# A scan's output in two passes with the next layer's row transform in the same stream, and that layer's first half transformed back beside its second half's items

## The chip, the cores and the metric

The kernel runs on one core of one Trainium2 chip. The metric is device time in microseconds (us), the median of the runs of one kernel.

## The reference, cut to what matters

Four layers follow each other on one image of 48 x 48 tokens with 768 channels, all in float32: attention with an MLP, a Fourier layer, a scan over 12 iterations, and a second Fourier layer. The change touches the last step of the scan and the second Fourier layer.

```python
# end of the scan layer
Hg = C_rot * Hst
Ho = transpose(Hg).reshape(B, H, W, R * N)          # R * N = 256
x = silu(Ho @ W_out + b_out)                        # 256 -> 768
# second Fourier layer
xs = rfft2(x, axes=(1, 2))                          # along h and w
# 8 blocks of 96 channels: two complex products with relu between, softshrink
x = irfft2(out_c, s=(H, W), axes=(1, 2)) + x
```

## The kernel before, in words

Tile code builds the kernel: the program is written as a sequence of operations on tiles, a scheduler orders them on each engine by the place where they are written and by the buffers that come free, and it inserts the waits. The order of each engine is then fixed.

**Scan output (`scan_phase`, lines 1223 to 1246).** The state `hg` has positions along w on the partitions; one column of `NPR` = 24 holds a pair of image rows. For two pairs at a time (`p2`, 12 rounds) four PE transposes (L1234) write a PSUM tile `ht`, ScalarE copies it to `hT` (L1236), and then for each of the two pairs and each half of the 768 channels (384 each) two matmuls (L1243, tile `so`, two passes each in the records) are followed by the addition of the bias on VectorE (L1245, tile `st`) and Silu on ScalarE into `x3` (L1246). `x3` has 96 partitions (two image rows of 48), 24 pairs and 768 channels. PSUM is split into two banks for `ht` and six for `so`.

**Second Fourier layer (`afno_second`, from L1561).** It has its own pools, opened when the scan's are closed. First, `spectrum_rows` (L1353) transforms along w: for each half of the channels and each of six groups of four pairs, four matmuls with the constant `fw` (L1361, tile `f_f`), four copies out of PSUM (`Evac`, L57 on ScalarE and L59 on VectorE in turn) into `ys` (two buffers), and one store of `ys` to DRAM, `yu[half]`, issued by SP (L1363).

Then `spectrum_mix` (L1366) loads its parameters (six of them, SP), sums two of them on GpSimd (L1402, L1403), and works through 40 items: two halves, five chunks of five frequencies (`kc`), four blocks of 96 channels. For each chunk it loads `yt` from `yu` (L1393, three buffers) and at the chunk's end stores `us` into the same place of `yu` (L1477). An item has four stages, each a few steps behind the one before: `s_fft_h` (five matmuls L1420 into `f_x`, copy L1422 on ScalarE, sum L1424 on GpSimd), `s_mlp1` (three matmuls L1434 to L1436, VectorE and ScalarE work, L1445 on GpSimd), `s_mlp2` (ten matmuls L1455 and L1456, two VectorE operations L1459 and L1461) and `s_ifft_h` (one matmul L1470 and a copy into `us`). A step of the loop runs them for four different items, in this way:

```python
stages = {s_ifft_h: 4, s_mlp2: 3, s_mlp1: 1, s_fft_h: 0}
for step in range(len(items) + 4):
    for stage, behind in stages.items():
        if 0 <= step - behind < len(items):
            stage(step - behind)
    beside(step)
```

`beside` is a callback; the first Fourier layer uses it for other work, the second gives one that does nothing. After all items, the transform back along w runs (L1582 to L1594): for each half and each of six groups, `load_spectrum` reads four pairs of `yu[half]` into `gt` (L1491, four buffers, SP); a group needs the `us` of all five chunks of its half. Four matmuls with `iw` follow (L1588, tile `f_w`), a VectorE addition onto `x3` in place (L1590) after each, and a store of four pairs to the output, issued by ScalarE (L1594). The last group of each half is stored pair by pair, from ScalarE and SP in turn (L1592). The scheduler places the first loads of the first half's `gt` ahead of the last items already, as far as the four buffers go; the matmuls on them stand behind the last item.

Of the kernel before, what the change touches and what calls it, by code (L numbers as in the profile page):

```python
# [11 lines left out]
F32 = mybir.dt.float32  # L12
BF16 = mybir.dt.bfloat16
AF = mybir.ActivationFunctionType
ALU = mybir.AluOpType
AX = mybir.AxisListType
PSUM = bass.MemoryType.PSUM
DRAM = bass.MemoryType.DRAM

P = 128  # L20
G = 48
# [7 lines left out]
TB = 384  # L29
NTB = T // TB  # L30
# [969 lines left out]
def scan_phase(tc, ident, w, w_close, wts, xT, xT_close, c_d, cr_d, out_open):  # L1000
# [7 lines left out]

    nc = tc.nc
    (b0_d, b1_d, cb_d, bands_d, wo_d, bo_d) = wts
    R4 = 3
# [8 lines left out]
    with tc.tile_pool(name="sc_s", bufs=1, side="left") as sp:  # L1022
# [202 lines left out]
        with (  # L1225
            tc.tile_pool(name="so_t", bufs=3, side="left") as tp,
            tc.tile_pool(name="so_q", bufs=2, space=PSUM) as pt,
            tc.tile_pool(name="so_p", bufs=6, space=PSUM) as pm,
        ):
            for p2 in range(NPR // 2):  # L1230
                ps = pt.tile([P, 512], F32, tag="t", name=f"ht_{p2}")
                for t in range(2):
                    for j in range(2):
                        nc.tensor.transpose(ps[:, (2 * t + j) * P : (2 * t + j) * P + K], hg[:K, 2 * p2 + t, j * P : (j + 1) * P], ident[:K, :K])  # L1234
                hT = tp.tile([P, 4, 2, G], F32, tag="hT", name=f"hT_{p2}")
                nc.scalar.copy(hT, ps.rearrange("p (i s w) -> p i s w", i=4, s=2)[:, :, :, :G])  # L1236
                for t in range(2):
                    pr = 2 * p2 + t
                    for half in range(2):
                        cols = slice(half * TB, (half + 1) * TB)  # L1240
                        ps = pm.tile([P, 512], F32, tag="m", name=f"so_{pr}_{half}")
                        for j in range(2):
                            nc.tensor.matmul(ps[:BS, :TB], lhsT=hT[:, 2 * t + j].rearrange("p s w -> p (s w)"), rhs=wo[:, j, cols], start=j == 0, stop=j == 1)  # L1243
                        t_ = tp.tile([BS, TB], F32, tag="t", name=f"st_{pr}_{half}")
                        V.tensor_tensor(t_, ps[:BS, :TB], bo[:, cols], ALU.add)  # L1245
                        nc.scalar.activation(x3[:, pr, cols], t_, AF.Silu)  # L1246
    return x3


def turn(eng, out, in_, co, si, m):  # L1250
# [12 lines left out]
def block_kernel(ctx: ExitStack, tc: tile.TileContext, a: dict):  # L1263
# [80 lines left out]
    wts = [a[k] for k in ("b_scan", "bias_scan", "conv_b", "bands", "W_out", "b_out")]  # L1344
    c_d = dram.tile([P, 8, NN * RR + 2 * NM, 3], F32, tag="c_d", name="c_d")
    cr_d = dram.tile([P, 8, NN * RR, 3], F32, tag="cr_d", name="cr_d")
    x3 = scan_phase(tc, ident, wsc, wsc_close, wts, x2T, x2T_close, c_d, cr_d, out_open)
    afno_second(tc, a, x3, yu)
    for close in reversed(closes):
        close()  # L1350

# [11 lines left out]
    nc.sync.dma_start(yu[half][:, 4 * g : 4 * g + 4, :], ys)  # L1363


def spectrum_mix(tc, name, a, layer, yu, psum, keep, side, halves, beside):  # L1366

# [2 lines left out]

    nc = tc.nc
    ev = Evac(nc)
    w1, b1, w2, b2 = (a[f"{layer}_{k}"] for k in ("w1", "b1", "w2", "b2"))
    HB = NB // 2
    with (
        tc.tile_pool(name=f"{name}_c", bufs=1, side=side) as cp,
        tc.tile_pool(name=f"{name}_y", bufs=3, side=side) as yp,
        tc.tile_pool(name=f"{name}_s", bufs=2, side=side) as sp,  # L1380
    ):
        fh = cp.tile([BS, BS], F32, tag="fh", name=f"{name}_fh")
        nc.sync.dma_start(fh, a["fh"])
        w1t = cp.tile([BS, NB, 2, BS], F32, tag="w1", name=f"{name}_w1")
        w1s, w1d = (cp.tile([BS, NB, BS], F32, tag=n, name=f"{name}_{n}") for n in ("w1s", "w1d"))
        w2t = cp.tile([BS + 1, NB, 2, BS], F32, tag="w2", name=f"{name}_w2")
        b1t = cp.tile([BS, 2, NB], F32, tag="b1", name=f"{name}_b1")
        ih = cp.tile([BS, BS], F32, tag="ih", name=f"{name}_ih")
        ys = {}

        def load(half, kc):
            yt = yp.tile([BS, KC, TB], F32, tag="yt", name=f"{name}_yt_{half}_{kc}")
            nc.sync.dma_start(yt, yu[half][4 * KC * kc : 4 * KC * (kc + 1)].rearrange("(k q) p c -> (q p) k c", q=4))  # L1393
            us = sp.tile([BS, KC, TB], F32, tag="us", name=f"{name}_us_{half}_{kc}")
            ys[half, kc] = yt, us

        nc.sync.dma_start(w1t, w1)
        nc.sync.dma_start(b1t, b1)
        nc.sync.dma_start(w2t[:BS], w2)
        nc.sync.dma_start(w2t[BS : BS + 1], b2)  # L1400
        nc.sync.dma_start(ih, a["ih"])
        nc.gpsimd.tensor_tensor(w1s, w1t[:, :, 0, :], w1t[:, :, 1, :], ALU.add)  # L1402
        nc.gpsimd.tensor_tensor(w1d, w1t[:, :, 1, :], w1t[:, :, 0, :], ALU.subtract)  # L1403

        o1s = []
        for i in range(3):
# [6 lines left out]
        def s_fft_h(i):  # L1413
            half, kc, b = items[i]
            if b == 0:
                load(half, kc)
            yt = ys[half, kc][0]
            ps = psum(f"x_{i}")
            for j in range(KC):
                nc.tensor.matmul(ps[:BS, j * BS : (j + 1) * BS], lhsT=yt[:, j, b * BS : (b + 1) * BS], rhs=fh, start=True, stop=True)  # L1420
            X = sp.tile([BS, 2, KC, G], F32, tag="X", name=f"{name}_X_{i}")
            nc.scalar.copy(X, ps[:BS, :CH].rearrange("c (k r h) -> c r k h", r=2, h=G))  # L1422
            Xs = sp.tile([BS, KC, G], F32, tag="Xs", name=f"{name}_Xs_{i}")
            nc.gpsimd.tensor_tensor(Xs, X[:, 0], X[:, 1], ALU.add)  # L1424
            flow[i] = X, Xs
# [103 lines left out]
def afno_first(tc, a, yu, x2T, follow_in, load_next):  # L1529

    nc = tc.nc
    ev = Evac(nc)
    x2v = x2T.rearrange("p c (h w) -> p c h w", w=HD)
    nc.gpsimd.memset(x2v[:, :, :, G:], 0.0)
    with (
        tc.tile_pool(name="f1_g", bufs=1, side="right") as gp,  # L1540
        tc.tile_pool(name="f1_p", bufs=8, space=PSUM) as pm,
    ):

        def psum(tag):
            return pm.tile([P, 512], F32, tag="m", name=f"f1_{tag}")

        iw = gp.tile([4 * KW, BS], F32, tag="iw", name="f1_iw")
        follow = follow_in(gp, 1)
        spectrum_mix(tc, "f1", a, "L1", yu, psum, True, "left", (1, 0), lambda step: follow(psum) if step in (1, 4) else load_next() if step == 8 else None)
        nc.sync.dma_start(iw, a["iw"])  # L1550
        for half in (1, 0):
            for g in range(NTB):
                gt = load_spectrum(nc, gp, yu, half, g, "f1", 3)
                for ct in range(NC // 2):
                    ps = psum(f"w_{half}_{g}_{ct}")
                    for i in range(4):
                        nc.tensor.matmul(ps[:, i * BS : (i + 1) * BS], lhsT=gt[: 4 * KW, i, ct * P : (ct + 1) * P], rhs=iw, start=True, stop=True)
                    ev(x2v[:, half * NC // 2 + ct, 8 * g : 8 * g + 8, :G], ps[:, :TB].rearrange("p (h w) -> p h w", w=G))


def afno_second(tc, a, x3, yu):  # L1561

    nc = tc.nc
    ev = Evac(nc)
    out = a["out"].rearrange("(p t) c -> t p c", t=BS)
    with (
        tc.tile_pool(name="f3_g", bufs=1, side="left") as gp,
        tc.tile_pool(name="f3_p", bufs=8, space=PSUM) as pm,
    ):
        fw = gp.tile([BS, YR], F32, tag="fw", name="f3_fw")  # L1570
        nc.sync.dma_start(fw, a["fw2"])
        iw = gp.tile([4 * KW, BS], F32, tag="iw", name="f3_iw")
        nc.sync.dma_start(iw, a["iw"])

        def psum(tag):
            return pm.tile([P, 512], F32, tag="m", name=f"f3_{tag}")

        for half in range(2):
            for g in range(NTB):
                spectrum_rows(nc, fw, x3[:, 4 * g : 4 * g + 4, half * TB : (half + 1) * TB], yu, half, g, psum, gp, ev, "f3")  # L1580
        spectrum_mix(tc, "f3", a, "L3", yu, psum, False, "left", (0, 1), lambda step: None)
        for half in range(2):  # L1582
            cols = slice(half * TB, (half + 1) * TB)
            for g in range(NTB):
                gt = load_spectrum(nc, gp, yu, half, g, "f3", 4)
                for i in range(4):
                    ps = psum(f"w_{half}_{g}_{i}")
                    nc.tensor.matmul(ps[:BS, :TB], lhsT=iw, rhs=gt[: 4 * KW, i, :], start=True, stop=True)  # L1588
                    dst = x3[:, 4 * g + i, cols]
                    nc.vector.tensor_tensor(dst, ps[:BS, :TB], dst, ALU.add)  # L1590
                    if g == NTB - 1:
                        (nc.scalar, nc.sync)[i % 2].dma_start(out[:, 4 * g + i, cols], dst)  # L1592
                if g < NTB - 1:
                    nc.scalar.dma_start(out[:, 4 * g : 4 * g + 4, cols], x3[:, 4 * g : 4 * g + 4, cols])  # L1594

# [109 lines left out]
```

## Time and profile before

| | us |
|---|---|
| median of 3 runs | 3879.38 (3878.82 to 3880.02) |
| the profiled execution | 3878.45 |
| its span, first to last instruction | 3876.6 |
| PE busy | 3761.5, 97% of the span |
| mean granted PE clock | 0.978 |
| stretch of the scan's output and what follows it | 3527 to 3876.6 |

PE matmul and PEld (its weight load) overlap, and matmul ends are modelled: two passes that follow each other overlap in the records, so the distance between starts is what a pass takes. Each instruction is named by engine, source line, operation, the tile it writes and those it reads, and its shape. "Idle before" names what ended the wait. DMA share is the mean busy share of the 16 DMA engines; a granted clock of 0.5 means that PE ran at half speed.

The stages can be followed by their first instructions: transposes of the scan's output at 3527.0, first `f_f` at 3598.8, first `f_x` of the items at 3634.5, last `f_o` at 3821.5, first `f_w` at 3830.75, last addition onto `x3` at 3872.8.

### The profile page before, as it was taken

The page shows a single profiled execution, that of the slowest core. Times are in us where ns is not written, and L with a number is a line of the kernel's source. Part 1 is how long each engine was busy: PE and PEld are TensorE (multiplying, and loading weights), DVE is VectorE, ACT ScalarE, POOL GpSimd, SP SyncE. Part 2 cuts the span into 40 slices and gives each one's busy share as a digit, 9 for nine tenths or more (in the row PEclk, how much of TensorE's full clock was granted, in tenths as well). Part 3 has the DMA queues.
Part 4 walks back from the last instruction along what each step waited for, and adds up shares of the span by engine and source line. Part 5 has one row for each costly group of instructions (what it writes and reads, how often), then busy time and mean ns, then how long its engine had stood idle before and what let it go on. Part 6 is the DMA issues. An engine that isn't in the chain of part 4 may idle for free. (4 is left out here: it accounts for less than half of the span.)

```text
span 3876.6 us, 54460 instructions
## 1 busy us (share of the span) xinstructions
PE 3761.5 (97%) x22018; PEld 2285.7 (59%) x22018; DVE 2059.0 (53%) x3185; ACT 1141.9 (29%) x1907; POOL 658.4 (17%) x496
## 2 busy tenths in 40 slices
PE   8999989999999999998999999999999998999998
PEld 4666544444444444455555555555568866996685
DVE  6655456666666666555425333232335367995355
ACT  1322244444444444421310120021023246223341
POOL 3101011111111111024000000000023301981131
PEclk9999989999999999999999999999999799999999
DMA  7656563424232322134334434433454302110444
GB/s 257 210 187 197 173 183 112 127 92 133 84 110 83 105 87 76 36 95 161 123 105 155 150 107 124 147 122 108 132 139 110 96 24 93 40 32 22 146 108 159
DMA packets 266810, 460.43 MB, mean 119 GB/s; under 512 B 32989, under 2 KB 219349, under 8 KB 260055
## 3 DMA queue, kind: packets, MB, share of 16 engines
q1 hardware_dynamic: 256919, 436.23, 36.3%
q10 hardware_dynamic: 9632, 20.65, 1.4%
q8 instruction: 175, 2.87, 0.3%
q14 instruction: 84, 0.69, 0.1%
HBM read 318.49 MB, written 138.31 MB: 118 GB/s over the span
## 5 line engine op out<-in xcount | busy, mean ns | idle before, releaser
L576 DVE TENSOR_TENSOR acc<-acc,p 128x768 f32<-128x768 f32 x576 | 582.8, 1012 | 354.9 <-ACT p L568 316.5
L568 ACT ACTIVATE p<-s 128x768 f32<-128x768 f32 x648 | 478.5, 812 | 692.7 <-PE s L566 580.5
L929 PE MATMUL p<-w,h 128*128 128x384 f32 x1512 | 492.7, 486 | 0.0
L558 PE MATMUL s<-qt,kv 64*128 64x384 f32 x2592 | 478.5, 501 | 9.1 <-ACT p L568 7.4
L587 PE MATMUL av<-p,kv 128*64 128x384 f32 x2592 | 464.5, 493 | 0.0
L929 PEld LDWEIGHTS p<-w,h 128*128 128x128 f32 x1512 | 286.1, 190 | 196.9
L558 PEld LDWEIGHTS s<-qt,kv 64*128 64x128 f32 x2592 | 233.1, 187 | 249.9 <-ACT p L568 116.0
L587 PEld LDWEIGHTS av<-p,kv 128*64 128x64 f32 x2592 | 170.0, 136 | 225.2 <-issue 215.8
L866 PE MATMUL p<-x2nT,w 128*128 128x384 f32 x864 | 294.0, 490 | 3.1 <-issue 3.1
L294 PE MATMUL qk<-xnT,wqk 128*128 128x384 f32 x756 | 252.5, 491 | 5.2 <-DMA wqk<-wqk_d 5.2
L1172 PE MATMUL c<-H,bands 128*48 128x96 f32 x5632 | 242.8, 247 | 12.1 <-issue 11.5
L566 PE MATMUL s<-bt,oneh 120*128 120x384 bf16 x1296 | 248.3, 328 | 0.0
L1172 PEld LDWEIGHTS c<-H,bands 128*48 128x48 f32 x5632 | 234.2, 123 | 20.9 <-issue 11.9
L866 PEld LDWEIGHTS p<-x2nT,w 128*128 128x128 f32 x864 | 165.4, 192 | 119.1 <-issue 6.0
L866 PE MATMUL p<-xT,w 128*128 128x384 f32 x648 | 220.8, 486 | 0.0
L566 PEld LDWEIGHTS <-oneh 120*128 120x128 bf16 x1296 | 109.1, 98 | 174.3 <-issue 115.1
L294 PEld LDWEIGHTS qk<-xnT,wqk 128*128 128x128 f32 x756 | 144.6, 193 | 99.9 <-issue 8.5
L905 POOL TENSOR_TENSOR rr<-rr,ml_b 128x1152 f32<-128x1152 f32 x12 | 33.5, 2788 | 954.4 <-DMA rr<-xr_d 660.8
L861 ACT ACTIVATE h<-h,ml_b 128x384 f32<-128x384 f32 x144 | 88.3, 614 | 346.6 <-DVE h L881 174.3
L1180 POOL TENSOR_TENSOR t<-s,c 128x768 f32<-128x768 f32 x80 | 144.8, 1836 | 214.3 <-DVE s L1142 203.8
L866 PEld LDWEIGHTS p<-xT,w 128*128 128x128 f32 x648 | 123.1, 190 | 85.9
L1082 PE MATMUL c<-wsc,x2T 128*112 128x357 f32 (+1 forms) x576 | 151.6, 426 | 2.0 <-DVE c L1043 2.0
(314 smaller groups left out, 4778.7 us busy)
## 6 DMA issues: line engine op xcount, KB each, us to landing
w<-w1s_d SPq DMA_DIRECT2D x36, 768.0 KB
w<-w2s_d SPq DMA_DIRECT2D x36, 768.0 KB
bt<-rh_d SPq DMA_DIRECT2D x144, 162.0 KB
w<-w1s_d SPq DMA_DIRECT2D x36, 576.0 KB
w<-in_mlp_w_dram SPq DMA_DIRECT2D x27, 768.0 KB
wqk<-wqk_d SPq DMA_DIRECT2D x12, 1344.0 KB
yu<-f_ys SPq DMA_DIRECT2D x24, 672.0 KB
f_gt<-yu SPq DMA_DIRECT2D x24, 672.0 KB
```

What stands on the lines that cost most here:

```text
L294: nc.tensor.matmul(p[:, :TB], lhsT=w[:, n, c, :], rhs=ops[sb][n][:, c, :], start=c == 0, stop=c == NC2 - 1)
L558: nc.tensor.matmul(ps[:, s, :QB], lhsT=keys[pr % 2][rows, kt * P : (kt + 1) * P], rhs=qbs[qc % 2][0][rows], start=True, stop=False)
L566: nc.tensor.matmul(ps[:, s, :QB], lhsT=oneh[:NBR, b % 3, :], rhs=qbs[qc % 2][1][:NBR, s, b // 3, j, :], start=False, stop=True)
L568: nc.scalar.activation(p, ps[:, :, :QB], AF.Exp)
L576: nc.vector.tensor_tensor(probs[c], probs[c], p, ALU.add)
L587: nc.tensor.matmul(avs[c][rows, :QB], lhsT=vals[pr % 2][:, kt, rows], rhs=p[:, s, :], start=kt == 0, stop=kt == NT - 1)
L861: nc.scalar.activation(h, h, AF.Gelu, bias=b1c[:, k : k + 1])
L866: nc.tensor.matmul(p[:, :TB], lhsT=w[n][:, c, :], rhs=rhs[n][:, c, :], start=c == 0, stop=c == NC2 - 1)
L929: nc.tensor.matmul(ps[t][:, :TB], lhsT=hs[left, f][:, t * P : (t + 1) * P], rhs=wt[:, f % KW2, :], start=f == 0, stop=f == NF2 - 1)
L1082: nc.tensor.matmul(ps[:K, i, :n], lhsT=xT[:, cc, tok : tok + K], rhs=w[:, cc, c0 : c0 + n], start=cc == 0, stop=cc == NC - 1)
L1172: nc.tensor.matmul(ps[r0 : r0 + G, k // 4, cols], lhsT=bands[:, n - GC, i, :] if gr else bands0[:, n, i, :], rhs=H[:, n, :, d : d + NPR], ...
L1180: GP.tensor_tensor(t, sc[:, ch], c1[:, m0 : m0 + GC].unsqueeze(2).to_broadcast([P, GC, RR, NPR]), ALU.mult)
```

## The change

**The scan's output in two passes.** `scan_phase` becomes a generator. The loop over halves goes outside the loop over `p2`: the first pass makes the 12 `hT` tiles (now each with a buffer of its own) and the first half of the channels; the second pass reuses them for the second half. After each `p2` of each pass it yields.

**The rows' transform in the same stream.** `afno_second` starts before the scan's output, opens its parameters and constants first (`spectrum_open`, the part of `spectrum_mix` that loaded them, now on the right side of memory), and at every second yield transforms one group of the rows that are finished, with the scan's six PSUM banks. While the second half's first three groups are transformed, it also writes the first half's three `yt` loads.

**The first half back within the items.** `beside` now loads the first half's `gt` from step 27 on and transforms its six groups back after steps 32, 35, 38, 40, 41 and 42 of 44. Behind the items only the second half's six groups remain. The pair-by-pair store is kept for the very last group alone.

```diff
@@ scan_phase
-            for p2 in range(NPR // 2):
...
+            yield x3, psum
+            hTs = []
+            for half in range(2):
+                cols = slice(half * TB, (half + 1) * TB)
+                for p2 in range(NPR // 2):
+                    if half == 0:
+                        ps = pt.tile([P, 512], F32, tag="t", name=f"ht_{p2}")
...
+                        hT = tp.tile([P, 4, 2, G], F32, tag=f"hT{p2}", name=f"hT_{p2}", bufs=1)
+                        nc.scalar.copy(hT, ps.rearrange("p (i s w) -> p i s w", i=4, s=2)[:, :, :, :G])
+                        hTs.append(hT)
+                    hT = hTs[p2]
+                    for t in range(2):
+                        pr = 2 * p2 + t
+                        ps = psum(f"{pr}_{half}")
                         for j in range(2):
                             nc.tensor.matmul(ps[:BS, :TB], lhsT=hT[:, 2 * t + j].rearrange("p s w -> p (s w)"), rhs=wo[:, j, cols], start=j == 0, stop=j == 1)
                         t_ = tp.tile([BS, TB], F32, tag="t", name=f"st_{pr}_{half}")
                         V.tensor_tensor(t_, ps[:BS, :TB], bo[:, cols], ALU.add)
                         nc.scalar.activation(x3[:, pr, cols], t_, AF.Silu)
-    return x3
+                    yield
@@ spectrum_open (new; the loads were in spectrum_mix)
+    cp, yp = (stack.enter_context(tc.tile_pool(name=f"{name}_{n}", bufs=bufs, side=side)) for n, bufs in (("c", 1), ("y", 3)))
...
+    def load(half, kc):
+        if (half, kc) not in yts:
+            yts[half, kc] = yp.tile([BS, KC, TB], F32, tag="yt", name=f"{name}_yt_{half}_{kc}")
+            nc.sync.dma_start(yts[half, kc], yu[half][4 * KC * kc : 4 * KC * (kc + 1)].rearrange("(k q) p c -> (q p) k c", q=4))
+        return yts[half, kc]
@@ afno_second
+    x3, scan_psum = next(scan)
+    with ExitStack() as stack:
+        opened = spectrum_open(tc, stack, "f3", a, "L3", yu, "right")
...
+        ready = [(half, g) for half in range(2) for g in range(NTB)]
+
+        def rows_in(n, psum):
+            half, g = ready[n]
+            spectrum_rows(nc, fw, x3[:, 4 * g : 4 * g + 4, half * TB : (half + 1) * TB], yu, half, g, psum, gp, ev, "f3")
+            if NTB <= n < NTB + 3:
+                opened[1](0, n - NTB)
+
+        for n, _ in enumerate(scan):
+            if n and n % 2 == 0:
+                rows_in(n // 2 - 1, scan_psum)
+            if n == 4 * NTB - 1:
+                rows_in(2 * NTB - 1, scan_psum)
...
+        items = 2 * NKC * (NB // 2)
+        loads = {items - 13 + 2 * g: g for g in range(4)}
+        backs = {items - 8: 0, items - 5: 1, items - 2: 2, items: 3, items + 1: 4, items + 2: 5}
+
+        def beside(step):
+            if step in loads:
+                load(0, loads[step])
+            if step in backs:
+                g = backs[step]
+                back(0, g)
+                if g + 4 < NTB:
+                    load(0, g + 4)
+
+        spectrum_mix(tc, "f3", opened, yu, psum, False, "left", (0, 1), beside)
+        for g in range(4):
+            load(1, g)
+        for g in range(NTB):
+            back(1, g)
+            if g + 4 < NTB:
+                load(1, g + 4)
```

`back(half, g)` holds the four matmuls, additions and the store of one group, as they were in the loop before. `load` is `load_spectrum` with the same four buffers.

## The prediction

> **What bounds the kernel now.** The page first: TensorE (PE) is busy 97% of the span, so a saving has to be a PE wait, PE time at a low clock, or the end of the kernel where transfers decide. The change touches only what follows the scan's last step, so I asked for the stretches of that part. Columns: length, busy time of PE, weight load, VectorE, ScalarE and GpSimd with counts, granted clock, DMA share, GB/s.
>
> ```profile
> core 0: us, PE busy (x) PEld busy (x) DVE busy (x) ACT busy (x) POOL busy (x), PEclk, DMA share, GB/s
> 3527.00:3599.00 72.00, 69.97 (x239) 36.81 (x240) 29.33 (x54) 30.63 (x61) 0.00 (x0) 0.97 0.01 2
> 3599.00:3631.00 32.00, 31.57 (x96) 16.49 (x95) 11.21 (x22) 9.81 (x23) 3.58 (x2) 1.00 0.79 244
> 3631.00:3635.00 4.00, 0.49 (x3) 0.53 (x4) 0.34 (x1) 0.15 (x1) 0.00 (x0) 0.81 1.00 378
> 3635.00:3652.00 17.00, 14.17 (x69) 12.04 (x69) 3.52 (x8) 5.24 (x12) 3.64 (x5) 0.54 0.50 143
> 3652.00:3821.00 169.00, 168.98 (x1406) 142.37 (x1405) 84.48 (x167) 70.53 (x167) 54.12 (x74) 1.00 0.33 87
> 3821.00:3831.00 10.00, 7.04 (x50) 4.87 (x49) 4.42 (x9) 1.56 (x4) 0.81 (x1) 1.00 0.01 2
> 3831.00:3877.00 46.00, 35.74 (x96) 16.55 (x94) 27.19 (x49) 0.00 (x0) 0.00 (x0) 0.88 0.86 290
> ```
>
> Read down: the scan's output (`so`) and the transform of rows (`f_f`) fill PE; then 4 us without PE work at a DMA share of 1.00; then 17 us at clock 0.54; then items that fill PE wholly; a drain with holes; and 46 us in which DMA is 0.86 busy. So the middle is PE's, the two edges are not. The chain of waits gives the edges and the rate between them (start, length, what):
>
> ```profile
> 3541.27 10.56 PE so L1243 x32
> 3552.84 10.56 PE so L1243 x32
> ...
> 3634.51 1.90 PE f_x L1420 x10
> ...
> 3652.08 0.85 PE f_x L1420 x10
> 3656.65 0.85 PE f_x L1420 x10
> ```
>
> One item takes 4.57. A 384-wide pass takes (10.56 - 0.49)/31 = 0.325, and a pair of transposed blocks has a period of 11.57. Last, the chain at the end, and two rows of the timeline that show its clock and the drain's holes:
>
> ```profile
> 3830.91 14.61 PE f_w L1588 x40
> ...
> 3846.13 13.96 DMA out_dram<-x
> ...
> 3860.16 7.40 DMA f_gt<-yu
> ...
> 3867.69 5.13 PE f_w L1588 x8
> ```
>
> ```profile
> 3825.62 1.05 PE L1470 MATMUL f_u<-f_Z,f_ih 96*96 96x480 f32 x2 [1.44 <-DVE f_Z L1461]
> ...
> 3829.89 1.02 PE L1470 MATMUL f_u<-f_Z,f_ih 96*96 96x480 f32 x2 [1.53 <-DVE f_Z L1461]
> ```
>
> The last eight passes need 5.13, 0.64 each: half speed, after 4.7 us of idleness.
>
> **What the skill says.** "TensorE: Matmul & The Clock Gate", section What's actually happening: an idle window of about 3.4 us halves the clock and a busy one restores it. The trace agrees on the fall (granted clock 0.50 after PE's 3.7 us wait at 3630.8), not on the recovery: it stayed at 0.50 until 3651.7, because the items' first steps leave PE holes of 1.4 us. Same page, section Architectural detail: ScalarE and VectorE take their instructions strictly in order; that decides what a waiting store on ScalarE's queue blocks. "DMA: Bandwidth & Descriptors", section Issuing engines are not separate DMA queues: stores issued by ScalarE share the 16 engines with SP's; the trace agrees (372 GB/s for both together at 3845 to 3861).
>
> **Part by part.** I follow the built program's order of instructions on each engine and put the durations of before beside it.
>
> *Stream.* The PE instructions are the same: 48 transposes, 192 `so` passes, 96 `f_f` passes. Before, they run from 3527.0 to 3630.8, 103.8. Removed: 0.3 between each of six pairs (11.57 less 32 passes and 0.93 of transposes), 1.9; and about 1.1 of waits in the rows (0.7 at their start for the last Silu, the rest for `yu` stores). Added: in the first pass each hT serves 8 passes (2.6) where it served 16, so the chain transpose, ScalarE copy (0.48), matmul lies open more often. In order, the copies stand behind Silus. I count 1.5 for the first three blocks, where three sets of transposes stand ahead of the first rows, and 0.5 for each of four later pairs: 3.5. Bounds: 1 if PE's queue hides it, 8 if each of twelve blocks pays 0.7. In the second pass rows follow a whole further pair (2.6 of cover for 0.55 add, 0.52 Silu and hops of 0.2): nothing; without that cover it would cost about 2 per group. Sum: the stream ends at 3527.0 + 103.8 - 3.0 + 3.5 = 3631.3.
>
> *Loads.* The eight parameter loads (1.3 MB) move ahead of SP's first `yu` store. They wait for the scan's last VectorE step (3526.9), and at 250 to 370 GB/s are down by about 3534; the first `f_f` stands at about 3540. On GpSimd, two sums move into its empty time. The three `yt` loads move between the `yu` stores of the second half; SP blocks for about 5 on the first half's last store, the next one is 7.7 behind. `ys` has two buffers, a store every 8 instead of every 2.7: that wait goes. Cost nothing, hidden by the stream; uncovered it would be the 3.7 of before.
>
> *Items' start.* The 3.7 wait for `yt` goes. Late next: the new PSUM pool takes over the stream's banks, so the first `f_x` waits for the last copies, 0.2 + 0.56 and a hop: 0.9. So `f_x` at 3632.2, 2.3 earlier. From there to steady took 16.2 at half clock (to 3650.7). At full clock the same chain is two rounds of 2.45 (`f_x`, copy, GpSimd sum) and 1.2 (`f_o`), then `f_x` 0.85 and `f_z` 1.7: 9.85. The two holes remain; before, the two like holes of the drain were followed by 3.4 at half clock (0.66 mean clock in 3831 to 3836). I take 12.0, bounds 9.9 and 16.2. Steady work is reached at 3644.2, 6.5 earlier.
>
> *First half back within the items.* 48 passes. Three groups fall in full items: 3 x 8 x 0.325 = 7.8, all on the path, since PE has no holes there. Their four VectorE adds (0.55 each) pass in front of nothing that PE needs within 2.5. The out store waits on ScalarE for the last add, 0.8 after the group; behind it is `f_both`, needed only after `f_u` 0.8, `f_z` 1.7 and `f_o`: nothing, else about 1 each. DMA share was 0.33 there; 7.7 MB more over 190 us is 40 GB/s. The `gt` loads on SP (one waits for a buffer of the first group) stand ahead of `us` stores that are ready later. Three groups fall in the drain, which was 9.3 and becomes pure PE work: 3 x 2.6 + 3 x 0.81 + 2 x 1.70 = 13.6, 4.3 more. The last `f_u` ends at 3830.8 - 6.5 + 7.8 + 4.3 = 3836.4.
>
> *Tail.* Before, 45.8: 12 groups back, DMA-bound. Now six, but their loads cannot start before the last `us` store has landed, and the first half no longer covers that. From the last `f_u`: copy 0.85, store down at 5.0 (traffic 3832.4 to 3835.5 before), 1.0 until the load's data flow, 0.69 MB at 370 GB/s 1.9, 0.9 until the matmul: 8.8. PE has been idle for that long, so about 7 of the first 8 passes at half clock: 4.8. Five groups 13.0, last add 0.75, last store to the end 3.2 (3873.4 to 3876.6): 30.5. Bounds: DMA alone, 7.67 MB at 372 GB/s is 20.6, with 6.0 ahead and 1.5 behind 28; half clock throughout 44. End: 3866.9, or 9.7 less.
>
> The profiled execution took 3878.45, 1.85 more than its span; the median shown is 0.93 above it. I put the difference on the median: 3879.38 - 9.7 = 3869.7. About 0.2% (7.8) is what this measurement tells from no change.
>
> **Rivals.** (1) The clock holds over the items' start (9.9) and DMA bounds the tail (28): 4.6 less, 3865; with a stream without holes 3863. For it: the stream ends busy. Against: the two holes. (2) The first pass pays 0.7 at each block and the start remains at half clock half as long as before (14): 4.5 + 2, 3876. For it: transposes ahead of the order, copies behind Silus, 1.9 between PE's `so` and VectorE after each pair already now. (3) Slower: the rows' transform waits for the Silu of its own pair each time, in both passes; 0.2 + 0.55 + 0.2 + 0.52 and the ScalarE queue, 2 per group, 12 groups: 24, so 3893. It decides from 1.5 per group. Against: another pair's 2.6 of matmuls stands between in the order; for it: three engines in strict order with six PSUM banks, where before the two jobs ran apart. That the move isn't made is excluded: in the built order the groups stand between the items.
>
> **Chances.** Forecast 0.50 (3865 to 3875), rival 1 0.20, rival 2 0.22, rival 3 0.08. Faster by over 0.2% is below 3871.6: rival 1 and about three quarters of the forecast, 0.58; the rest of it and rival 2 within, 0.34; slower 0.08. The range 3860 to 3879 leaves out rival 3 and the ends of the first two, under 0.2.
>
> **What would show it.** `f_x` starting near 3632 and PE's clock at 1.00 by 3645; items with a group at 7.2 instead of 4.57; no 1.4 holes in the drain; first `f_w` of the second half about 9 after the last `f_u`, slow for one group. I am wrong if the stream ends after 3636, if items without a group slow down, or if the tail exceeds 34.

## The result, and the profile after

The changed kernel takes 3872.39 us (median of 4 runs, 3870.29 to 3873.58) where the kernel before took 3879.10 beside it: a ratio of 0.9982, 95% interval 0.9965 to 0.9999. That is 6.7 us or 0.17%, just inside the 0.2% named as the limit of what can be told from no change, though the interval stays below 1. Measured again later, with 14 runs, the ratio was 0.9984 (0.9976 to 0.9992). The profiled execution took 3872.97 with a span of 3871.2: 5.4 less span than before.

The stages of the changed kernel, in the columns that the prediction explained:

```profile
3527.00:3630.00 103.00, 101.35 (x334) 53.73 (x334) 40.29 (x74) 41.26 (x85) 3.59 (x2) 0.98 0.37 109
3630.00:3645.00 15.00, 11.36 (x63) 9.92 (x64) 3.89 (x10) 4.13 (x9) 3.63 (x5) 0.66 0.15 47
3645.00:3775.00 130.00, 129.98 (x1079) 109.51 (x1078) 65.88 (x129) 53.64 (x127) 40.97 (x56) 1.00 0.38 100
3775.00:3823.00 48.00, 48.00 (x361) 37.78 (x360) 26.18 (x51) 17.31 (x41) 13.16 (x18) 1.00 0.35 104
3823.00:3837.00 14.00, 14.00 (x73) 8.40 (x71) 10.41 (x20) 1.59 (x4) 0.80 (x1) 1.00 0.30 85
3837.00:3849.00 12.00, 0.57 (x2) 0.39 (x2) 0.65 (x1) 0.00 (x0) 0.00 (x0) 0.59 0.79 223
3849.00:3871.00 22.00, 17.32 (x48) 8.22 (x46) 13.29 (x24) 0.00 (x0) 0.00 (x0) 0.89 0.93 287
```

Against the table of before: the 4 us without PE work at DMA share 1.00 are gone, the start at a low clock is shorter but still there (0.66 over 15 us), the drain (3823 to 3837) has no holes, and in place of one DMA-bound tail of 46 there are 12 us in which PE does next to nothing, and 22 for the second half. The chain of waits of the changed kernel has its lengths:

```profile
3629.62 1.14 issue
3630.76 1.07 PE f_x L1436 x10
...
3779.20 0.85 PE f_x L1436 x10
3780.04 2.58 PE f_w L1627 x8
...
3786.35 0.85 PE f_x L1436 x10
...
3837.84 5.34 DMA yu<-f_us
...
3843.25 5.21 DMA f_gt<-yu
...
3848.51 17.82 PE f_w L1627 x48
```

An item with a group takes 3786.35 - 3779.20 = 7.15 instead of 4.57: the group's 2.58 lies wholly on the path. Between the last `f_u` (ends at 3837.1) and the second half's first `f_w` stand a store of 5.34 and then a load of 5.21. After that 48 passes take 17.82; at 0.325 each they would take 15.6.

| step, us | before | predicted | after |
|---|---|---|---|
| end of the stream | 3630.8 | 3631.3 | 3629.6 |
| first `f_x` | 3634.5 | 3632.2 | 3630.8 |
| from there to steady items | 16.2 | 12.0 | 14.2 |
| end of the last `f_u` | 3830.8 | 3836.4 | 3837.1 |
| last `f_u` to the second half's first `f_w` | - | 8.8 | 11.4 |
| its 48 passes | - | 17.8 | 17.8 |
| last pass to the end | - | 3.95 | 4.9 |
| tail, the last three together | 45.8 | 30.5 | 34.1 |
| end | 3876.6 | 3866.9 | 3871.2 |

### The profile page after: what moved, and what is told of

It is laid out like the page before. It is cut to its first block, busy times and chain, and to the rows that moved or that the text cites. A ratio compares the mean times of both kernels' runs of the same rounds, so it can differ in the third digit from the quotient of the medians.

```text
span 3871.2 us, 54411 instructions
## 1 busy us (share of the span) xinstructions
PE 3755.7 (97%) x22018; PEld 2284.7 (59%) x22018; DVE 2060.4 (53%) x3185; ACT 1142.1 (30%) x1907; POOL 657.5 (17%) x496
## 4 chain that ended last, share of the span: by engine, by line
PE 90%; DVE 4%; DMA 2%; ACT 1%; issue 1%; POOL 1%; SPq 1%; ACTq 0%; DVEq 0%; POOLq 0%
PE p L866 13%; PE p L929 13%; PE s L558 12%; PE av L587 11%; PE qk L294 6%; PE s L566 6%; PE c L1084 4%; PE c L1174 3%; PE v L163 3%; PE pj L163 2%; PE f_z L1471 2%; PE f_z L1472 2%; PE f_x L1436 2%; PE f_u L1486 2%; PE so L1254 2%; PE f_w L1575 2%
## 5 line engine op out<-in xcount | busy, mean ns | idle before, releaser
L1174 PE MATMUL c<-H,bands 128*48 128x96 f32 x5632 | 242.1, 247 | 11.7 <-issue 11.5
```

The costliest lines, as they stand in the source:

```text
L1174: nc.tensor.matmul(ps[r0 : r0 + G, k // 4, cols], lhsT=bands[:, n - GC, i, :] if gr else bands0[:, n, i, :], rhs=H[:, n, :, d : d + NPR], ...
```

## The experiments

The theory after this profile: the stream makes the gain (its start of the items is 5.7 us earlier), while the back part only pays for itself, 7.8 + 4.3 us of PE work against 11.7 us of tail. What is left to win is at the two edges: the items' start, and the tail's store, load and low clock. The rivals: the back part is worth 3 us as predicted; the tail ends when DMA's bytes are through, whatever PE does.

The traces differ from run to run by some us before the first `so` matmul of the scan's output (it stands between 3522.8 and 3528.7), where no edit reaches. So traces are compared from that matmul to the end of the span; ratios are to the kernel before on the same chip. Two ratios are drawn down by a single run each, 3842.3 among the 19 with 14 idle matmuls and 3830.9 among the 6 of the last row; their medians give 0.9982 and 0.9949.

| kernel | first `so` to end | from the end of the last `f_u` | ratio (95%) |
|---|---|---|---|
| before | 348.1 | 45.8 | 1 |
| changed | 342.5, again 343.1 | 34.1, again 35.3 | 0.9982 (0.9965 to 0.9999), again 0.9984 (0.9976 to 0.9992) |
| stream only | 343.7 | 45.4 | 0.9983 (0.9975 to 0.9991) |
| back only | 348.4 | 35.2 | 0.9999 (0.9989 to 1.0008) |
| four groups held | 339.9 | 38.9 | 0.9982 (0.9976 to 0.9989) |
| two groups held | 338.3 | 33.1 | 0.9976 (0.9968 to 0.9985) |
| rows late | 335.4 | 34.7 | 0.9967 (0.9954 to 0.998) |
| load cut in two | 340.9 | 32.9 | 0.9978 (0.997 to 0.9987) |
| 14 idle matmuls | 343.2 | 35.6 | 0.9975 (0.9967 to 0.9984) |
| 18 idle matmuls | 340.9 | 32.9 | 0.998 (0.9974 to 0.9987) |
| three edits | 330.4 | 32.3 | 0.9954 (0.9941 to 0.9966) |
| three edits, ordered | 333.5 | 32.3 | 0.9959 (0.9946 to 0.9972) |
| the same with 5 idle matmuls | 328.1 | 29.8 | 0.9939 (0.9916 to 0.9962) |

### Each part of the change alone

Stream only, against the changed kernel:

```diff
-            last = half == 1 and g == NTB - 1
+            last = g == NTB - 1
...
-        loads = {items - 13 + 2 * g: g for g in range(4)}
-        backs = {items - 8: 0, items - 5: 1, items - 2: 2, items: 3, items + 1: 4, items + 2: 5}
+        loads, backs = {}, {}
...
-        for g in range(4):
-            load(1, g)
-        for g in range(NTB):
-            back(1, g)
-            if g + 4 < NTB:
-                load(1, g + 4)
+        for half in range(2):
+            for g in range(NTB):
+                load(half, g)
+                back(half, g)
```

> The two passes with the rows' transform in the stream, but all twelve groups transformed back after the items, in the loop of before. Theory (the stream makes the whole gain, the first half within the items pays for itself and no more): steady items 5.7 us earlier than before (3645.0 against 3650.7), drain with its two holes of about 1.5 again, tail of 45.8 again: 5 to 6.5 us faster than before, about 3873, and within 1.5 us of the full change. Rival (as the prediction had it, the back part is worth 3.2 of its own): 3 us or more slower than the full change, 3875 to 3877.

Back only, against the kernel before (`load`, `back` and `beside` as in the changed kernel):

```diff
-        spectrum_mix(tc, "f3", a, "L3", yu, psum, False, "left", (0, 1), lambda step: None)
-        for half in range(2):
...
+        spectrum_mix(tc, "f3", a, "L3", yu, psum, False, "left", (0, 1), beside)
+        for g in range(4):
+            load(1, g)
...
```

> The stream of before (scan's output whole, then the rows' transform by itself), and the first half back within the items as in the changed kernel. Theory: 7.8 us for three groups in full items and 4.3 for three in the drain are added, and the tail falls from 45.8 to 34.1, 11.7 less: +0.4, so 3879 to 3880, no change. Rival (the prediction's tail of 30.5): 3.2 us faster than before, 3876.

Measured: 0.9983 for the stream alone, as much as the change's 0.9982 to 0.9984, and 0.9999 for the back part alone. These times don't settle it by themselves: the 3.2 us of the prediction would be 0.9992, inside the interval of the back part alone. The traces side with the theory: the stream alone gains 4.4 us and the back part costs 0.3, where the changed kernel's own two profiles gain 5.6 and 4.9. The back part alone adds its 12.1 us of PE work and takes 10.6 from the tail; its start of the items is 1.4 shorter. So the 3.2 us are nowhere seen, though a gain of 1 or 2 can't be excluded. The stages of the stream-only kernel show where its time lies:

```profile
3627.00:3643.00 16.00, 12.04 (x66) 10.48 (x67) 4.61 (x12) 4.17 (x10) 3.64 (x5) 0.68 0.14 44
3809.00:3824.00 15.00, 11.82 (x79) 8.54 (x78) 5.58 (x11) 3.56 (x8) 2.27 (x3) 0.85 0.05 17
3824.00:3869.50 45.50, 35.72 (x97) 16.46 (x95) 27.23 (x49) 0.00 (x0) 0.00 (x0) 0.88 0.86 293
```

The start is as in the changed kernel, the drain has its holes again (11.82 of 15), and the tail has its DMA share of 0.86 at 293 GB/s over 45.5 us, as before the change.

### The items' start: real work into PE's holes

The last three groups of the rows' transform leave the stream and stand behind the first three steps of the items:

```diff
-            if n and n % 2 == 0:
+            if n and n % 2 == 0 and n // 2 - 1 < 9:
                 rows_in(n // 2 - 1, scan_psum)
-            if n == 4 * NTB - 1:
-                rows_in(2 * NTB - 1, scan_psum)
...
         def beside(step):
+            if step < 3:
+                rows_in(9 + step, psum)
```

> The changed kernel with the last three groups of the rows' transform moved out of the stream and behind the first three steps of the items, where PE has holes. Theory (the items' start costs 8.6 us of holes and half clock, and both go when PE has other work there): stream ends 7.8 earlier, items steady at the same 15 to 16 us after it at full clock: 6 to 8 us faster than the changed kernel, about 3865. Rival (the clock falls for the 1.1 us wait between stream and items, whatever follows): holes go but the half clock stays for 10 us or so, gain of 0 to 3 us.

Measured: ratio 0.9967, and 7.1 us less than the changed kernel's first profile from the first `so` matmul on, 7.7 less than its second. The theory holds. First the timeline of the changed kernel there, then that of this one:

```profile
3630.76 1.06 PE L1436 MATMUL f_x<-f_fh,f_yt 96*96 96x96 f32 x10 [1.14 <-issue]
3633.27 0.65 PE L1450 MATMUL f_o<-f_Xs,f_w 96*96 96x240 f32 x2 [1.45 <-POOL f_Xs L1440]
...
3638.04 1.11 PE L1450 MATMUL f_o<-f_Xs,f_w 96*96 96x240 f32 x2 [1.43 <-POOL f_Xs L1440]
```

```profile
3618.66 1.09 PE L1436 MATMUL f_x<-f_fh,f_yt 96*96 96x96 f32 x10 [0.71 <-DVE st L1256]
3619.59 2.76 PE L1372 MATMUL f_f<-x,f_fw 96*112 96x384 f32 x8
3622.18 0.57 PE L1450 MATMUL f_o<-f_Xs,f_w 96*96 96x240 f32 x2
```

In the changed kernel PE waits 1.14, 1.45 and 1.43 us, and the same `f_o` matmuls take 0.65 and then 1.11 where they need 0.57: the clock was 0.50 from about 3634 to 3644. With eight `f_f` passes in each hole there is no wait behind the first `f_x`, and the granted clock is 1.00 throughout. So more than half of the 7.1 to 7.7 us is not the waits themselves, of which 4.0 fell to 0.7, but the clock after them. The rival's first wait is 0.7 here and not 1.1; but in the changed kernel the clock fell only 3.5 us after the end of that wait, behind the second. The three later versions with the rows late have full clock there too.

### The tail: what stands between the halves

Four groups of the first half are held back as work for the 11.4 us gap (five `gt` buffers instead of four):

```diff
-        loads = {items - 13 + 2 * g: g for g in range(4)}
-        backs = {items - 8: 0, items - 5: 1, items - 2: 2, items: 3, items + 1: 4, items + 2: 5}
+        loads = {items - 13 + 2 * g: g for g in range(NTB)}
+        backs = {items - 8: 0, items - 5: 1}
...
-        for g in range(4):
-            load(1, g)
+        for g in range(2, NTB):
+            load(1, g - 2)
+            back(0, g)
```

> The changed kernel with two groups of the first half within the items and the other four (2 to 5) after the last item, ahead of the second half; five gt buffers, so the four are loaded before. Theory (PE idles 11.4 us at the store and load between the two, and then runs slowly; four groups of 2.6 fit into that): last f_u 4.3 + 2.6 = 6.9 us earlier, the second half's first f_w still about 11.4 after it, its 48 passes in 15.6 instead of 17.8: about 9 us faster than the changed kernel, near 3863.5. Rival (the tail is bound by DMA): the four held groups' out stores, 2.4 MB or 6.3 us at 372 GB/s, stand in the way of the store and the loads, so that the gap grows to about 17.5 and the gain is about 3 us, near 3869.5.

Measured: ratio 0.9982, no better than the change; in the trace 2.7 us less than its first profile. The rival is nearer, though the gap is 12.9 and not its 17.5. The last `f_u` did end 7.4 us earlier, but the tail grew from 34.1 to 38.9:

```profile
3829.00:3842.00 13.00, 12.62 (x34) 5.84 (x32) 9.30 (x17) 0.00 (x0) 0.00 (x0) 0.87 0.70 198
3842.00:3859.00 17.00, 16.35 (x48) 7.42 (x48) 13.04 (x25) 0.00 (x0) 0.00 (x0) 1.00 1.03 345
3859.00:3868.00 9.00, 0.00 (x0) 0.00 (x0) 0.46 (x1) 0.00 (x0) 0.00 (x0) 0.77 0.79 260
```

In the second stretch PE is busy and at full clock and DMA is at a share of 1.03 with 345 GB/s; when PE is done at 3859 the stores need 9 us more. Here DMA's bytes set the end: 10.8 MB moved in this tail, against 9.0 in that of the changed kernel.

Two held groups, 4 and 5:

```diff
-        backs = {items - 8: 0, items - 5: 1, items - 2: 2, items: 3, items + 1: 4, items + 2: 5}
+        backs = {items - 8: 0, items - 5: 1, items - 2: 2, items: 3}
...
         for g in range(4):
             load(1, g)
+            if g < 2:
+                back(0, 4 + g)
```

> The changed kernel with groups 4 and 5 of the first half moved from the drain to behind the last item (buffers as in the changed kernel). The bytes of the tail are almost those of the changed kernel, since their two stores lay behind the last f_u there too. Theory (four held groups failed because of their 2.4 MB of stores alone): last f_u 3.1 us earlier, first f_w of the second half still about 12 after it, last pass to the end 5 to 6: 2 to 3.5 us faster than the changed kernel. Rival (any store in the gap stands in the way of the store and loads of the second half): gap of 14 as with four held groups, gain under 1 us.

Measured: ratio 0.9976, 4.2 us less than the changed kernel's first profile; more than the theory's 2 to 3.5, and the rival's 14 us gap isn't there (10.3). Only one of the two stores had lain behind the last `f_u` in the changed kernel: 9.6 MB moved in this tail against 9.0. PE now waits only 5.2 us, yet the 48 passes still took 17.64: with half of the gap filled the clock still fell.

The load after the store cut in two, with five buffers:

```diff
+        early = 4 * KC * (NKC - 1)
+        def load_first(g):
+            gts[1, g] = bp.tile([YR, 4, TB], F32, tag="gt", name=f"f3_gt_1_{g}", bufs=5)
+            nc.sync.dma_start(gts[1, g][:early], yu[1][:early, 4 * g : 4 * g + 4, :])
+        def load_rest(g):
+            nc.sync.dma_start(gts[1, g][early : 4 * KW], yu[1][early : 4 * KW, 4 * g : 4 * g + 4, :])
...
+                if g >= 2:
+                    load_first(g - 2)
...
         for g in range(4):
-            load(1, g)
+            load_rest(g)
```

> The changed kernel with the second half's first four gt loads cut in two: the 80 rows of the first four chunks are loaded while the items drain, and only the 20 rows of the last chunk wait for its us store; five gt buffers instead of four. About 2 MB of 9 leave the tail, and the load after the store has 0.12 MB instead of 0.69. Theory (the tail's gap is a store and then a load, each with its bytes): load 2.5 to 3.5 instead of 5.2, gap of 11.4 down to 9, end 3 to 5 us earlier than in the changed kernel. Rival (the gap is a fixed latency, whatever the bytes): gap stays at 11, end within 1 us. If the early loads delay the last us store, it lands later than 5.3 us after its issue.

In this kernel the first of the early loads stands one step ahead of the fourth chunk's store and so reads that chunk's rows before they are written: its output is wrong there, while the sizes of the transfers are as meant. Its chain of waits:

```profile
3834.48 5.37 DMA yu<-f_us
...
3839.86 2.76 DMA f_gt<-yu
...
3842.76 18.79 PE f_w L1636 x48
```

With 0.12 MB instead of 0.69 the load takes 2.76 instead of 5.21: the gap has a part that goes with the bytes, and it falls from 11.4 to 9.0. The end came only 1.6 us earlier than in the changed kernel's first profile, less than expected, since the passes took 18.79, 1.0 more. DMA's share during them was 0.79 and the granted clock 0.83: this tail was held up by PE's clock.

### The clock in the tail by itself

Idle matmuls, which nobody reads, between the last `f_u` and the first `f_w`:

```diff
         for g in range(4):
             load(1, g)
+        for n in range(14):
+            ps = psum(f"warm_{n}")
+            nc.tensor.matmul(ps[:BS, :TB], lhsT=fw[:, :BS], rhs=x3[:, n, :TB], start=True, stop=True)
```

> The changed kernel with fourteen matmuls more, which nobody reads, between the last f_u and the second half's first f_w (9.1 us at 0.65 each, in a gap of 11.4). Nothing of the result changes. Theory (half clock costs the tail 2.2 us): the 48 passes take 15.6 to 15.9 instead of 17.8 and the end comes 1.5 to 2.2 earlier than in the changed kernel. Rival (the tail ends when DMA is done): the passes are as much faster, but from the last pass to the end it takes 6.5 to 7 us instead of 4.9, and the end comes at most 0.5 earlier.

Both expectations failed: the 48 passes took 18.61, not 15.6. The stages of this kernel say why; read the third number from the right, the granted clock:

```profile
3844.00:3846.00 2.00, 1.31 (x5) 0.35 (x3) 0.00 (x0) 0.00 (x0) 0.00 (x0) 1.00 0.86 246
3846.00:3848.00 2.00, 0.00 (x0) 0.00 (x0) 0.00 (x0) 0.00 (x0) 0.00 (x0) 0.78 1.02 289
3848.00:3850.00 2.00, 1.92 (x3) 0.96 (x4) 0.32 (x1) 0.00 (x0) 0.00 (x0) 0.50 1.04 289
```

The idle matmuls ended 2.8 us before the data came, and that was enough: the clock fell while PE waited, and stayed at 0.50 until about 3854. So four more of them:

```diff
-        for n in range(14):
+        for n in range(18):
```

> The changed kernel with eighteen idle matmuls instead of fourteen in the tail's gap (11.7 us), so that no wait of 3 us is left ahead of the first f_w. Nothing of the result changes. With fourteen, 2.8 us of waiting were left and the 48 passes still took 18.6. Theory: at full clock 15.6 to 16 for the 48 passes; if the clock sets the tail, it takes 32 us instead of 34.1. Rival (DMA sets the end: 4.1 MB of loads, 3.5 of stores and what is left from before): the passes wait for loads or the stores lag, and the tail stays within 0.7 us of 34.1.

Now the chain reads:

```profile
3834.59 11.61 PE f_warm L1653 x36
3846.20 15.49 PE f_w L1627 x48
```

15.49 us at a clock of 1.00. The tail is 32.9, which is 1.2 less than in the changed kernel's first profile and 2.4 less than in its second, while the medians (0.998 against 0.9984) can't be told apart. Theory and rival both hold a part: from the last pass to the end it took 5.8 us instead of 4.9, and DMA had a share of 1.03 during the passes (1.01 in the changed kernel). The likely reading is that PE's clock and DMA's bytes lie within some 2 us of each other in this tail, so that taking one away shows little.

### Together

Rows late, groups 4 and 5 held, and three of the second half's loads cut in two (two of them read rows too early here, as above; `rows_in` as in the version with rows late, `load_first` and `load_rest` as in the one with the load cut in two):

```diff
-        backs = {items - 8: 0, items - 5: 1, items - 2: 2, items: 3, items + 1: 4, items + 2: 5}
+        backs = {items - 8: 0, items - 5: 1, items - 2: 2, items: 3}
...
+                if g >= 1:
+                    load_first(g - 1)
...
+        for g in range(3):
+            load_rest(g)
+        for g in range(4, NTB):
+            back(0, g)
         for g in range(NTB):
+            if g + 3 < NTB:
+                load(1, g + 3)
             back(1, g)
```

> All three together: the last three row groups behind the first steps of the items, groups 4 and 5 of the first half behind the last item, and three of the second half's gt loads cut in two, with five buffers. If the gains add: 7.3 (measured for the rows) + 2 to 3 + 3 to 4 faster than the changed kernel: 3858 to 3860 where the changed kernel has 3871. If tail gains don't add because DMA's bytes set the end: 9 us faster, 3862.

Measured: 330.4 us from the first `so` matmul, 12.1 less than the changed kernel's first profile. One by one the three edits gave 7.1, 4.2 and 1.6, so the gains nearly add. The 48 passes took 18.55 after a wait of 3.4. Then with the early loads behind the fourth chunk's store:

```diff
-                if g >= 1:
-                    load_first(g - 1)
+            if step == items:
+                for g in range(3):
+                    load_first(g)
```

> The version with all three edits, with the early loads of the second half's gt put behind the store of the fourth chunk (in the version before they stood one step ahead of it and read those rows too early). Theory: from the first output matmul to the end 331 to 332 us, as before the mending, against 342.5 in the changed kernel: 10 to 12 us faster than it. Rival: the loads, which now come together at step 40, delay the last us store by 2 us or more, so that 1 to 2 us of the gain are lost.

Measured: 333.5, ratio 0.9959 (0.9946 to 0.9972). The loads don't delay the last `us` store: SP issues the loads that wait for it 4.3 us after it, in this version and in the one before. The 3 us more than in the version before stand elsewhere: 1.5 in the stream, whose first 10 us had a granted clock of 0.66 against 0.84, and 1.6 in the drain, where the clock fell to 0.71 behind two holes of 1.5 us, while the other version has the same drain at 1.00. The edit touches neither place; differences of 1 to 2 us between two of these traces are no finding. Last, five idle matmuls in the wait that was left:

```diff
         for g in range(4, NTB):
             back(0, g)
+        for n in range(5):
+            ps = psum(f"warm_{n}")
+            nc.tensor.matmul(ps[:BS, :TB], lhsT=fw[:, :BS], rhs=x3[:, n, :TB], start=True, stop=True)
```

> The version before, with five matmuls that nobody reads (3.25 us) in the 3.4 us that PE waits ahead of the second half's first f_w. Theory (a wait of about 3 us is enough to halve PE's clock for 5 to 6 us): the 48 passes take 15.6 to 16 instead of 18.5, and the end comes 2 to 3 us earlier, since DMA has slack there. Rival (DMA's bytes bound the tail by now): the passes are faster, the end comes less than 1 us earlier.

```profile
3821.76 5.16 PE f_w L1634 x16
3826.92 3.23 PE f_warm L1667 x10
3830.15 15.68 PE f_w L1634 x48
```

Measured: ratio 0.9939 (0.9916 to 0.9962); 328.1 us from the first `so` matmul, 20 less than before and 14 to 15 less than the changed kernel. The 48 passes took 15.68, 2.8 to 2.9 less than in the two versions before, and the end moved with them (tail 29.8 instead of 32.3): DMA had the slack that the held groups and the cut loads gave it. The other 2.9 of the 5.4 us between this version and the one before lie in the two places named there, which this edit doesn't touch either. This version beats both kernels.

The changed kernel itself was measured beside the last three:

> The changed kernel itself on this chip, as the measure for the three others: 6 to 7 us faster than the kernel before, as in its first measurement.

It was 0.9984 of before, 6.6 us less.

## Why the prediction was right, and where it wasn't

The predicted time was 3869.7, measured 3872.39, inside the range of 3860 to 3879. That range reached almost to the time of before, so lying inside it says little. Of the 9.7 us forecast, 6.7 came (5.4 in the profiled span), and the case called likeliest for the verdict, faster by over 0.2%, missed by 1.1 us.

**Stream: right, its stalls too large.** It was to end 0.5 us later and ended 1.2 earlier. In the changed kernel PE is idle 1.65 us between 3527 and 3630 in all, so the first pass's open chain of transpose, copy and matmul cannot cost more than that; the prediction took 3.5. (Its removed 1.9 is too large as well: 11.57 less 32 passes of 0.325 and 0.93 is 0.24, which makes 1.4 for six.) Rival 3, the rows waiting for their own pair's Silu, isn't there: in the second pass rows and `so` passes follow each other without a gap in the chain.

**Wait for `yt`: right.** It goes, and in its place comes one of 1.14 (0.9 forecast).

**Items' start: mechanism right, size off.** 12.0 forecast, 14.2 measured, 12.8 in the changed kernel's second profile. The two holes stayed, as the prediction said, and kept the clock down for 10.2 us in the first profile and 6.8 in the second, not for the 3.4 after them that it took over from the drain of before. The experiment with rows there shows that filling the holes was worth 7 us.

**Groups in full items and in the drain: right.** 7.15 per item with a group, no holes in the drain; the last `f_u` 0.7 later than forecast, all of it from the start.

**Tail: the term that failed is 8.8 from the last `f_u` to the first `f_w`.** It was 11.4, and 11.4 again in the second profile. Its two parts, the store and the load, were each too small.

The store was to be down 5.0 after the last `f_u`, and the load was issued at 6.1. The 5.0 came from the kernel before, where DMA had nothing else to move. But 9.0 MB pass in this tail, not 7.67: the `us` store itself has 0.74, and the out store of the first half's last group, 0.59, is issued at 3836.9, just ahead of it. The packets show the order: those of the out store pass from 3837.5 to 3840.3, those of the `us` store from 3839.8 to 3842.7, though it was issued at 3837.84. In the versions with four groups held and with three edits no out store stands ahead of it, and it takes 4.17 and 4.23 instead of 5.34. The chain of the version with three edits:

```profile
3824.33 4.23 DMA yu<-f_us
```

From the issue of the load to the matmul the forecast had "1.0 until the load's data flow, 0.69 MB at 370 GB/s 1.9, 0.9 until the matmul", 3.8, and it took 5.3. No out store moves beside it; the other three loads, issued within 1.3 us behind it, do. Whether they are what the missing 1.5 went to is not shown.

The skill's page "DMA: Bandwidth & Descriptors", section Anatomy of one DMA, gives 2.0 us and the bytes at 436 GB/s, fitted for transfers that GpSimd issues; for the 0.74 MB store and the 0.69 MB load an estimate from it is 3.7 and 3.6. The trace has 5.3 and 5.2 with other traffic beside them, 4.2 for the store with none ahead of it, and 2.76 for a load of 0.12 MB; the measurement decides.

The end after the last pass took 4.9, not 3.95: DMA was still at a share of 1.00 from 3866.5 to 3869, where in the kernel before it was at 0.28 after the last pass. The 17.8 for the 48 passes was right to the tenth in this profile, but that is luck: the second has 18.9.

So the sum: stream -1.7, `f_x` wait +0.2, start +2.2, tail +2.6 and +0.95 make +4.3, the difference between the predicted span end and the measured one. The two large errors are in the back part's tail and the start's clock; the stream's error, the other way, hides part of them. With a tail of 34.1 the back part is worth nothing, 7.8 + 4.3 - 11.7, and the run with it alone agrees: 0.3 us more in the trace, 0.9999 in the times. The prediction's own mark for being wrong, a tail beyond 34, was just met.

Why the same waits made the items' start 14.2 us long in one profile and 12.8 in the other can be read from the recorded changes of the granted clock. From 3500 us on they stand a whole multiple of 3.41 us apart in every trace. Eight traces have the same first two waits here, 1.14 to 1.15 and 1.45. Where the clock fell 3.1 to 3.5 us after the first `f_x` (four traces) it stayed low for 10.2 us and the start took 14.2; where it fell after 4.0 to 4.3 (three traces), for 6.8 us, and the start took 12.7 to 12.8; in one it fell twice for 3.4, and the start took 13.4. So what the same waits cost goes with how they lie against these steps of 3.41, and that differs from run to run. The same holds ahead of all edits: after the first `so` matmul the clock stayed low for 1.8 us in one trace and for 4.8 in another, which at half speed makes 1.5 us. What stays open is how much idle time within a step makes the clock fall.

## What to carry to other kernels

Work that is moved out of a tail onto a full engine is paid in full there; it gains only if the tail doesn't get a new wait, so look for the store-then-load that the moved work had covered, and for a store that is issued just ahead of it. Where PE has short holes, look for real work that exists already to fill them: here three groups of eight passes did it, and more than half of what the holes had cost was the clock after them. What follows a last store can be cut into a part that is loaded before it and a small rest; here that made the gap 2.4 us shorter, but the end came only 1.6 earlier, since the clock still fell in the wait that was left.

## What the runs showed of the hardware

- Ahead of the second half's first `f_w` PE waited between 2.8 and 11.4 us in nine profiles, and the 48 passes that followed took 17.6 to 19.1 us in all of them, with no order by the length of the wait. With no wait, or one of 0.9 us, they took 15.5 to 16.4. So a wait of 2.8 us cost as much as one of 11.4.
- The skill's page "TensorE: Matmul & The Clock Gate", section HAM oscillation — how this bites in real kernels, puts the limit at idle gaps above about 3.4 us. Here a gap of 2.8 us was enough (with 14 idle matmuls the clock fell 1.8 us into it), and at the items' start two waits of 1.14 and 1.45 with 1.1 us of work between them. In the kernel before, the clock fell at 3633.5, 2.7 us into the wait of 3.7 that the prediction put ahead of the fall.
- In those nine tails, in work without holes, the clock came back 3.9 to 6.7 us after the first pass. At the items' start, with holes of 1.4 us in the work, it stayed down for up to 10.2 us, and for 17.1 in the kernel before (to 3650.5, not the 3651.7 that the prediction names).
- A full DMA does not always move the same: during the second half's 48 passes its share was 1.01 to 1.03 in the changed kernel and in those with 18 idle matmuls, four groups held and two groups held, at 311, 333, 345 and 350 GB/s.
